# Stages behind a scan start at its second block of channels and load block by block; the last image's stage joins the list

## The chip, the cores and the metric

The kernel runs on one core of one Trainium2 chip. It computes four images in one launch. The metric is the device time in microseconds (us) of that core, as the median over runs; lower is better. TensorE is called PE here, VectorE DVE, ScalarE ACT, GpSimd POOL, and SyncE SP. SP does no arithmetic: it issues the DMAs.

## The reference

Four layers follow each other. Only layers 0 and 3 hold a scan over the 1024 positions of an image; the layers between are a grouped convolution, a masked attention and a mixture of experts. `x` is (4, 32, 32, 256). Cut to what matters for the change:

```python
# layer 0: 512 channels, 64 states, per image
x = layernorm(src) @ w_in; x = gelu(depthwise_conv3x3(x))
dt = softplus(dt_raw @ w_dt + dt_bias)
def step(h, inp):
    xt, dtt, Bt, Ct = inp
    dA = exp(dtt[:, :, None] * A)
    h = dA * h + (dtt * xt)[:, :, None] * Bt[:, None, :]
    return h, einsum('bdn,bn->bd', h, Ct)
_, ys = scan(step, h0, xs)
y = layernorm(ys + x * D_skip)
out = src + (y @ w_out + b_out)

# layer 3: 512 channels, 16 states, per image; its scan has the same form
y = y_seq * silu(x_gate)
t = t + (y @ W_out + b_out)
t = t + moe(layernorm(t))        # 8 experts, the best two of a token kept
```

The change concerns what stands between the scan and its use: the product with `D_skip` and the projection in layer 0, the product with the gate and the projection in layer 3.

## The kernel before

**Units and blocks.** A scan is cut into four blocks `d` of 128 channels, each into two halves `c` of 64 channels. States and channels together fill the 128 partitions: a unit is a tile of 128 rows by 1024 positions, with two channels of 64 states in layer 0 (64 units to a block, 256 to an image) or eight channels of 16 states in layer 3 (16 and 64). The list `SCANS` runs the eight scans one after the other, image 0 and 1 of layer 0, image 0 of layer 3, image 2 of layer 0, image 1 of layer 3, image 3 of layer 0, images 2 and 3 of layer 3: 1280 units, numbered 0 to 1279 here. `scans` (line 345) is a generator that writes them down: for unit k, SP loads the decay `dA` of unit k + 4 (line 410; two DMAs of 256 KB in layer 0, eight of 64 KB in layer 3, into one of five buffers), PE spreads the inputs of unit k + 1 (`ps_rep`), ACT takes the exponential of unit k + 2, DVE multiplies by B and scans, POOL multiplies by C, and PE sums pairs of units over the states (`ps_y`). When a half is summed, ACT copies it out and SP stores it to DRAM in two DMAs (line 464). When the last half of the last block is stored, the scan is put into the set `done` (line 466).

**Stages.** All other work is written as generators that stand in the list `STAGES` (line 33): `front` (layer 0 up to its scan), `middle` (line 1694: `back0`, layers 1 and 2, and layer 3 up to its scan) and `last` (line 1704: `back3` and the last experts). The third entry names the scan that has to be done first. `advance` (line 507) runs the current stage up to its next `yield`; when none is open it takes the first of the list whose scan is in `done`. Only one stage is open at a time.

**How they are interleaved.** The scheduler's own ordering is switched off while the scans run (`manual_schedule`), so each engine gets its instructions in the order in which Python writes them. After each half of a unit `run` (line 521) calls `advance` up to twice, as long as no engine's estimated clock is ahead of DVE's (`LEAD`, `LAG`, `TICKS`, line 45). The value of a `yield` is a note only: `advance` passes it on, but nothing adds it up. If a scan needs inputs that no stage has produced yet, `need` (line 494) advances stages without a scan until they are there.

**What a stage does behind its scan.** `scanned` (line 754) allocates the tile `y_back` and loads it with eight DMAs of 256 KB. `back0` (line 761) loads the residual `tb` (1 MB), `y_back`, four blocks of `u_back` (512 KB each) and `w_out` (512 KB) one behind the other; after two empty yields POOL adds a bias to `tb`, DVE adds `u * D_skip` to each of the four blocks (the skip instructions), PE transposes `y_back` for the layernorm's sums and then projects it. `back3` (line 1641) does the same with `gate_back` for `u_back`; here POOL multiplies y by the gate in eight pieces, then adds the bias.

**The last image.** Its last stage isn't in the list. When all stages are done, `run` opens a new PSUM pool and writes `last(3)` there, outside `manual_schedule`, so that the scheduler orders it.

**Buffers.** The tiles of the stages come from a stack of pools on the right side of SBUF. A new stage takes the memory of the one that has ended, so its first loads wait for the last readers of that memory, a store to DRAM among them. All loads and stores named here go through SP's one queue, in order.

Of the kernel before, what the change touches and what calls it, by code (L numbers as in the profile page):

```python
# [7 lines left out]
F32 = mybir.dt.float32  # L8
# [5 lines left out]
PSUM = bass.MemoryType.PSUM  # L14
DRAM = bass.MemoryType.DRAM

P = 128
NB = 4
L = 1024
TB = L // P  # L20
C = 256
DI = 512
DC = DI // P
# [9 lines left out]
STAGES = (  # L33
    ("front", 0, None), ("front", 1, None), ("front", 2, None), ("front", 3, None), ("middle", 0, (0, 0)),
    ("middle", 1, (0, 1)), ("middle", 2, (0, 2)), ("middle", 3, (0, 3)), ("last", 0, (3, 0)),
    ("last", 1, (3, 1)), ("last", 2, (3, 2)),
)
SAFE = 40.0
SORTS = 2
AHEAD = 12  # L40
# [49 lines left out]
class Metered:  # L90
# [21 lines left out]
    def __getattr__(self, key):  # L112
        got = getattr(self.what, key)
        if self.name is None:
            return Metered(got, self.clock, key) if key in self.COST else got
        cost = self.COST[self.name].get(key)
        if cost is None:
            return got

        def run(*args, **kw):  # L120
            self.clock[self.name] += cost(*args, **kw)
            return got(*args, **kw)  # L122

        return run


class Hybrid:
# [217 lines left out]
    def scans(self, mp, psum):  # L345
# [7 lines left out]
        nc = self.nc  # L353
# [9 lines left out]
        y = None  # L363
# [77 lines left out]
        def pair(k):  # L441

            nonlocal y
            scan, d, c, i, j = units[k]
            n = self.states[scan[0]]
            per = 32 * n // P
            collect = self.tables[scan[0]][2]
            if i == 0:
                y = psum.tile([P, 512], F32, tag="y", name="ps_y", bufs=1)
            h = [state.pop(k - 1), state.pop(k)]  # L450
            for g in range(2):
                for j in range(2):
                    at = 32 * (2 * g + j)
                    nc.tensor.matmul(
                        y[at : at + 32, :], lhsT=collect[:, i, :],
                        rhs=h[j][:, g * 512 : (g + 1) * 512],
                        start=(i == 0), stop=(i == per - 1), tile_position=(0, at),
                    )
            if i == per - 1:
                yo = mp.tile([P, 512], F32, tag="yo", name="yo", bufs=2)  # L460
                nc.scalar.copy(yo, y)
                to = self.keep(("y", *scan, d, c), [64, L])
                for g in range(2):
                    nc.sync.dma_start(to[:, g * 512 : (g + 1) * 512], yo[64 * g : 64 * g + 64, :])
                if d == DC - 1 and c == 1:
                    self.done.add(scan)

        for k in range(AHEAD):
            chunk(k)
# [37 lines left out]
    def advance(self):  # L507

        if self.stage is None:
            can = [x for x in self.todo if x[2] is None or x[2] in self.done]  # L510
            if not can:
                return None
            self.todo.remove(can[0])
            self.stage = getattr(self, can[0][0])(can[0][1])
        cost = next(self.stage, None)
        if cost is None:
            self.stage = None
            return 0.0
        return cost

    def run(self):

        self.done, self.ready = set(), set()
        self.todo, self.stage = list(STAGES), None
        nc, tc = self.nc, self.tc
        with tc.tile_pool(name="scan", bufs=1) as mp, tc.tile_pool(
            name="scps", bufs=1, space=PSUM
        ) as psum, tc.tile_pool(name="sdps", bufs=1, space=PSUM) as side, tc.manual_schedule():
            self.side_psum(side)
            self.mask_work, self.sorted = self.mask_prepare(), False  # L530
            clock = self.clock = dict.fromkeys(Metered.COST, 0.0)
            self.nc = Metered(nc, clock)
            for n, _ in enumerate(self.scans(mp, psum)):
                if n % 2:
                    next(self.mask_work, None)
                now = clock["vector"]
                for e in clock:
                    clock[e] = max(clock[e], now - LAG)
                for _ in range(TICKS):
                    if max(clock.values()) > clock["vector"] + LEAD or self.advance() is None:  # L540
                        break
            while self.advance() is not None:
                pass
            self.nc = nc
        assert not self.todo
        with tc.tile_pool(name="lps", bufs=2, space=PSUM) as pp:
            self.side_psum(pp)
            for _ in self.last(NB - 1):
                pass

# [198 lines left out]
    def image(self, flat, b):  # L751
        return flat[b * L : (b + 1) * L, :].rearrange("(j p) c -> p j c", p=P)

    def scanned(self, pool, key):
        y = pool.tile([P, DC, L], F32, name="y_back")
        for d in range(DC):
            for c in range(2):
                self.nc.sync.dma_start(y[64 * c : 64 * c + 64, d, :], self.mem["y", *key, d, c])
        return y

    def back0(self, b, tb):

# [1 line left out]
        nc, tc, vec = self.nc, self.tc, self.vec  # L764
        with tc.tile_pool(name=f"k{b}", bufs=1, side="right") as sp:
            nc.sync.dma_start(tb, self.image(self.a["x"].rearrange("b h w c -> (b h w) c"), b))
            y = self.scanned(sp, (0, b))
            u = sp.tile([P, DC, L], F32, name="u_back")
            for d in range(DC):
                nc.sync.dma_start(u[:, d, :], self.mem["u", 0, b, d])  # L770
            w_out = sp.tile([P, DC, C], F32, name="w_out0")
            nc.sync.dma_start(w_out, self.mem[("w_out0",)])
            yield 2.0
            yield 2.0
            yield from self.add_rows(tb, self.bout0, TB)
            for d in range(DC):
                nc.vector.scalar_tensor_tensor(
                    y[:, d, :], u[:, d, :], vec["L0_conv_D_skip"][:, d : d + 1], y[:, d, :],
                    ALU.mult, ALU.add,
                )  # L780
                yield 1.3
            mv = sp.tile([P, TB, 2], F32, name="b0mv")
            got = {}

# [856 lines left out]
    def back3(self, b, tb):  # L1641
        nc, tc = self.nc, self.tc
        with tc.tile_pool(name=f"h{b}", bufs=1, side="right") as sp:
            nc.sync.dma_start(tb, self.mem["t", b])
            y = self.scanned(sp, (3, b))
            gate = sp.tile([P, DC, L], F32, name="gate_back")
            for d in range(DC):
                nc.sync.dma_start(gate[:, d, :], self.mem["gate", b, d])
            w_out = self.weight(sp, "L3_attn_W_out", DC)
            yield 2.0  # L1650
            yield 2.0
            for d in range(DC):
                for g in range(2):
                    cols = slice(g * 512, (g + 1) * 512)
                    nc.gpsimd.tensor_tensor(y[:, d, cols], y[:, d, cols], gate[:, d, cols], ALU.mult)
                    yield 0.8
            yield from self.add_rows(tb, self.bout3, TB)
            got = {}

            def project(j):  # L1660
# [95 lines left out]
```

## Time and profile before

| What | Value |
|---|---|
| median of 3 runs | 6912.75 us (6912.15 to 6918.07) |
| the profiled execution's own time | 6914.57 us |
| its span, first to last instruction | 6912.9 us |
| granted TensorE clock, mean | 0.822 |
| DVE busy in 3847 to 3893 us (scan alone) | 43.41 of 46 us |
| DVE busy in 3893 to 3925 us (a middle stage begins) | 18.65 of 32 us, DMA engines 0.91 busy |
| SP's loads of `dA` | 2048 of 256 KB and 2048 of 64 KB |
| last instruction of the scans ends | about 6480 us |

A page of the profile gives busy time and instruction counts by engine over the span of one execution. A timeline line gives start and length in us, the engine, the line of the code, the operation, what it writes and reads, the shapes, how many instructions are merged, and in brackets how long the engine had stood idle before it and what ended that. `SPq` lines are DMAs being issued; when their data lands is not in them. Line 122 stands for everything that goes through the wrapper that keeps the estimated clocks, so most of the work carries it, and the tiles' names tell the instructions apart. In the list of waits at a tile, a line gives the releaser, the idle time in us and how often it occurred.

### The profile page before, as it was taken

Reading aid. Unit: us, or ns where it says so; the run is one execution under the profiler, and the core shown is the slowest. Engines: PE = TensorE matmul, PEld = TensorE weight load, DVE = VectorE, ACT = ScalarE, POOL = GpSimd, SP = SyncE. Lnnn points to the kernel's source line nnn. Section 1 sums busy time; section 2 is a strip of 40 time slices with the busy share of each in tenths; the row PEclk is TensorE's granted clock in tenths of the full one; section 3 lists DMA queues with packets and bytes.
Section 4 is the critical chain, followed back from the end, with each engine's and each line's share of the span. In section 5 each row is a group of like instructions: output and inputs, shape, how many; then the busy total and the mean of one; then the engine's idle time right before and its main releaser. Section 6 shows DMA issues by size and latency. Waiting matters only on the chain. (4 is left out here: it accounts for less than half of the span.)

```text
span 6912.9 us, 66308 instructions
## 1 busy us (share of the span) xinstructions
PE 5388.0 (78%) x20516; PEld 2219.1 (32%) x20516; DVE 5204.9 (75%) x4477; ACT 3440.9 (50%) x4145; POOL 3644.9 (53%) x1801
## 2 busy tenths in 40 slices
PE   6558768678797567879689668798698678867979
PEld 3002212222342032234145322243253322523556
DVE  7778988877898986889889867898899840237411
ACT  2426667345476333457568334477386332244411
POOL 0876776755557654555856545557666530035200
PEclk8568768679898577989789779898698889877989
DMA  1556665654466665446656655456666630145321
GB/s 71 147 147 161 176 173 157 183 134 113 119 173 169 157 164 128 116 126 177 184 142 165 174 135 124 121 150 173 168 165 167 162 95 0 49 123 144 95 61 34
DMA packets 394239, 937.47 MB, mean 136 GB/s; under 512 B 83220, under 2 KB 165729, under 8 KB 392225
## 3 DMA queue, kind: packets, MB, share of 16 engines
q1 hardware_dynamic: 391696, 930.53, 51.1%
q8 instruction: 172, 2.82, 0.2%
q0 software_dynamic: 2128, 2.13, 0.2%
q14 instruction: 243, 1.98, 0.1%
HBM read 842.59 MB, written 93.95 MB: 135 GB/s over the span
## 5 line engine op out<-in xcount | busy, mean ns | idle before, releaser
L122 POOL TENSOR_TENSOR h<-h,rows 128x1024 f32<-128x1024 f32 x1280 | 3028.5, 2369 | 2002.5 <-DVE h L122 1620.7
L122 DVE TENSOR_TENSOR_SCAN h<-dA,ps_rep 128x1024 f32<-128x1024 f32 x1280 | 2924.6, 2285 | 209.8 <-issue 89.5
L122 DVE TENSOR_TENSOR ps_rep<-ps_rep,rows 128x1024 f32<-128x1024 f32 x1280 | 1553.3, 1213 | 336.3 <-PE ps_rep L122 313.8
L122 ACT ACTIVATE dA<-dA,A_L_conv_A_log 128x1024 f32<-128x1024 f32 x1024 | 1152.3, 1145 | 693.0 <-DMA dA<-dt 582.1
L122 PE MATMUL ps_rep<-S,spread_L_conv_A_log 96*128 96x512 bf16 x2048 | 755.7, 459 | 751.9 <-DVE h L122 696.0
L122 PE MATMUL ps_y<-h,collect_L_conv_A_log 128*32 128x512 f32 x4096 | 774.0, 750 | 104.3 <-POOL h L122 104.2
L122 ACT ACT_TABLE_LOAD x486 | 623.5, 1283 | 72.4 <-PE ps_h L122 49.9
L122 PEld LDWEIGHTS <-spread_L_conv_A_log 96*128 96x128 bf16 x2048 | 164.3, 103 | 1502.8 <-DVE h L122 1157.5
L122 PE MATMUL ps_h<-xTm,we 128*128 128x512 f32 x1280 | 605.7, 609 | 5.6 <-ACT h_m L122 4.5
L122 PE MATMUL ps_e<-we,h_m 128*128 128x256 f32 x2560 | 589.1, 382 | 6.8 <-ACT h_m L122 6.8
L122 ACT ACTIVATE p<-ps_sc 128x512 f32<-128x512 f32 x512 | 277.9, 594 | 588.7 <-PE ps_sc L122 558.6
L122 PEld LDWEIGHTS ps_e<-we,h_m 128*128 128x128 f32 x2560 | 483.2, 190 | 137.1 <-issue 46.7
L122 ACT ACTIVATE dA<-dA,A_L_attn_A_log 128x1024 f32<-128x1024 f32 x256 | 293.4, 1148 | 460.6 <-DMA dA<-dt 434.6
L122 PE MATMUL ps_at<-p,v 128*32 128x512 f32 x1024 | 361.6, 624 | 61.4 <-ACT p L122 53.3
L122 PE MATMUL ps_rep<-S,spread_L_attn_A_log 96*128 96x512 bf16 x512 | 188.8, 458 | 266.5 <-DVE h L122 220.9
L122 ACT ACTIVATE h_m<-ps_h,cols 128x512 f32<-128x512 f32 x320 | 217.0, 687 | 313.2 <-PE ps_h L122 310.4
L122 DVE SCALAR_TENSOR_TENSOR tb<-ps_e,cw,tb 128x256 f32<-128x256 f32 x448 | 192.6, 473 | 214.4 <-PE ps_e L122 214.4
L122 PEld LDWEIGHTS ps_h<-xTm,we 128*128 128x128 f32 x1280 | 242.5, 194 | 287.0 <-issue 238.7
L122 PE MATMUL ps_sc<-qT,kT 32*128 32x512 f32 x1024 | 301.8, 665 | 0.0
L122 PE MATMUL ps_at<-p,ones 128*32 128x512 f32 x1024 | 278.7, 624 | 0.0
L122 PE MATMUL ps_cv<-pad,diag 128*128 128x512 f32 x576 | 260.4, 593 | 0.0
L122 PEld LDWEIGHTS ps_y<-h,collect_L_conv_A_log 128*32 128x32 f32 x4096 | 101.3, 119 | 488.5 <-POOL h L122 240.3
(360 smaller groups left out, 5454.3 us busy)
## 6 DMA issues: line engine op xcount, KB each, us to landing
dA<-dt SPq DMA_DIRECT2D x2048, 256.0 KB
dA<-dt SPq DMA_DIRECT2D x2048, 64.0 KB
we<-in_L_ffn_W_dram SPq DMA_DIRECT2D x64, 512.0 KB
parts<-parts SPq DMA_DIRECT2D x64, 384.0 KB
S<-parts SPq DMA_DIRECT2D x96, 256.0 KB
dt<-sp_r SPq DMA_DIRECT2D x64, 256.0 KB
y<-yo SPq DMA_DIRECT2D x128, 128.0 KB
y_back<-y SPq DMA_DIRECT2D x64, 256.0 KB
```

The source lines that it names most:

```text
L122: return got(*args, **kw)
```

## The change

Five things are edited.

1. `done` takes a pair of scan and block when the second half of a block is stored, for every block.
2. `advance` looks for a stage whose scan has its last block done, and failing this for one whose scan has block `EARLY` = 1 done, so two blocks of four.
3. `scanned` no longer allocates; it loads one block (two DMAs), after it has yielded a `Wait` for that block. While a `Wait` isn't fulfilled, `advance` returns None and runs nothing, other stages included.
4. `back0` and `back3` load block by block: the block of u or gate, then the two y loads, then the product of the block before. The bias on `tb` comes right after the first block, `w_out` is loaded there too. Four yields stand between a block's loads and the product of the block before.
5. `last` of image 3 joins `STAGES`, and the separate ending of `run` is gone, with its PSUM pool.

```diff
@@ -33,8 +33,10 @@
 STAGES = (
     ("front", 0, None), ("front", 1, None), ("front", 2, None), ("front", 3, None), ("middle", 0, (0, 0)),
     ("middle", 1, (0, 1)), ("middle", 2, (0, 2)), ("middle", 3, (0, 3)), ("last", 0, (3, 0)),
-    ("last", 1, (3, 1)), ("last", 2, (3, 2)),
+    ("last", 1, (3, 1)), ("last", 2, (3, 2)), ("last", 3, (3, 3)),
 )
+
+EARLY = 1
 SAFE = 40.0
 SORTS = 2
 AHEAD = 12
@@ -122,6 +124,10 @@
             return got(*args, **kw)
 
         return run
+
+
+class Wait(tuple):
+    pass
 
 
 class Hybrid:
@@ -462,8 +468,8 @@
                 to = self.keep(("y", *scan, d, c), [64, L])
                 for g in range(2):
                     nc.sync.dma_start(to[:, g * 512 : (g + 1) * 512], yo[64 * g : 64 * g + 64, :])
-                if d == DC - 1 and c == 1:
-                    self.done.add(scan)
+                if c == 1:
+                    self.done.add((scan, d))
 
         for k in range(AHEAD):
             chunk(k)
@@ -507,21 +513,29 @@
     def advance(self):
 
         if self.stage is None:
-            can = [x for x in self.todo if x[2] is None or x[2] in self.done]
+            can = [
+                x for d in (DC - 1, EARLY) for x in self.todo
+                if x[2] is None or (x[2], d) in self.done
+            ]
             if not can:
                 return None
             self.todo.remove(can[0])
             self.stage = getattr(self, can[0][0])(can[0][1])
+        if self.wait and self.wait not in self.done:
+            return None
+        self.wait = None
         cost = next(self.stage, None)
         if cost is None:
             self.stage = None
             return 0.0
+        if isinstance(cost, Wait):
+            self.wait = tuple(cost)
         return cost
 
     def run(self):
 
         self.done, self.ready = set(), set()
-        self.todo, self.stage = list(STAGES), None
+        self.todo, self.stage, self.wait = list(STAGES), None, None
         nc, tc = self.nc, self.tc
         with tc.tile_pool(name="scan", bufs=1) as mp, tc.tile_pool(
             name="scps", bufs=1, space=PSUM
@@ -543,10 +557,6 @@
                 pass
             self.nc = nc
         assert not self.todo
-        with tc.tile_pool(name="lps", bufs=2, space=PSUM) as pp:
-            self.side_psum(pp)
-            for _ in self.last(NB - 1):
-                pass
 
 
 
@@ -751,12 +761,11 @@
     def image(self, flat, b):
         return flat[b * L : (b + 1) * L, :].rearrange("(j p) c -> p j c", p=P)
 
-    def scanned(self, pool, key):
-        y = pool.tile([P, DC, L], F32, name="y_back")
-        for d in range(DC):
-            for c in range(2):
-                self.nc.sync.dma_start(y[64 * c : 64 * c + 64, d, :], self.mem["y", *key, d, c])
-        return y
+    def scanned(self, key, y, d):
+
+        yield Wait((key, d))
+        for c in range(2):
+            self.nc.sync.dma_start(y[64 * c : 64 * c + 64, d, :], self.mem["y", *key, d, c])
 
     def back0(self, b, tb):
 
@@ -764,21 +773,34 @@
         nc, tc, vec = self.nc, self.tc, self.vec
         with tc.tile_pool(name=f"k{b}", bufs=1, side="right") as sp:
             nc.sync.dma_start(tb, self.image(self.a["x"].rearrange("b h w c -> (b h w) c"), b))
-            y = self.scanned(sp, (0, b))
+            y = sp.tile([P, DC, L], F32, name="y_back")
             u = sp.tile([P, DC, L], F32, name="u_back")
-            for d in range(DC):
+            w_out = sp.tile([P, DC, C], F32, name="w_out0")
+
+            def fetch(d):
                 nc.sync.dma_start(u[:, d, :], self.mem["u", 0, b, d])
-            w_out = sp.tile([P, DC, C], F32, name="w_out0")
-            nc.sync.dma_start(w_out, self.mem[("w_out0",)])
-            yield 2.0
-            yield 2.0
-            yield from self.add_rows(tb, self.bout0, TB)
-            for d in range(DC):
+                yield from self.scanned((0, b), y, d)
+
+            def skip(d):
                 nc.vector.scalar_tensor_tensor(
                     y[:, d, :], u[:, d, :], vec["L0_conv_D_skip"][:, d : d + 1], y[:, d, :],
                     ALU.mult, ALU.add,
                 )
+
+            yield 1.0
+            yield from fetch(0)
+            yield from self.add_rows(tb, self.bout0, TB)
+            nc.sync.dma_start(w_out, self.mem[("w_out0",)])
+            for d in range(1, DC):
+                yield from fetch(d)
+                for _ in range(4):
+                    yield 0.5
+                skip(d - 1)
                 yield 1.3
+            for _ in range(4):
+                yield 0.5
+            skip(DC - 1)
+            yield 1.3
             mv = sp.tile([P, TB, 2], F32, name="b0mv")
             got = {}
 
@@ -1642,19 +1664,31 @@
         nc, tc = self.nc, self.tc
         with tc.tile_pool(name=f"h{b}", bufs=1, side="right") as sp:
             nc.sync.dma_start(tb, self.mem["t", b])
-            y = self.scanned(sp, (3, b))
+            y = sp.tile([P, DC, L], F32, name="y_back")
             gate = sp.tile([P, DC, L], F32, name="gate_back")
-            for d in range(DC):
+
+            def fetch(d):
                 nc.sync.dma_start(gate[:, d, :], self.mem["gate", b, d])
-            w_out = self.weight(sp, "L3_attn_W_out", DC)
-            yield 2.0
-            yield 2.0
-            for d in range(DC):
+                yield from self.scanned((3, b), y, d)
+
+            def gated(d):
                 for g in range(2):
                     cols = slice(g * 512, (g + 1) * 512)
                     nc.gpsimd.tensor_tensor(y[:, d, cols], y[:, d, cols], gate[:, d, cols], ALU.mult)
                     yield 0.8
+
+            yield 1.0
+            yield from fetch(0)
+            w_out = self.weight(sp, "L3_attn_W_out", DC)
             yield from self.add_rows(tb, self.bout3, TB)
+            for d in range(1, DC):
+                yield from fetch(d)
+                for _ in range(4):
+                    yield 0.5
+                yield from gated(d - 1)
+            for _ in range(4):
+                yield 0.5
+            yield from gated(DC - 1)
             got = {}
 
             def project(j):
```

## The prediction

> **What bounds the kernel now.** I read the page first, then the waits at the tile `y_back` (the summed scan output that a stage loads back), then the timelines around each of its loads, and last the order in which the two built programs put instructions on each engine.
>
> ```profile
> PE 5388.0 (78%) x20516; PEld 2219.1 (32%) x20516; DVE 5204.9 (75%) x4477; ACT 3440.9 (50%) x4145; POOL 3644.9 (53%) x1801
> ```
>
> No engine is full over the span. The shape is a serial scan of 1280 units on DVE, each a multiply (1.21 us) and a scan (2.29 us), start to start 3.60 us where nothing else is on DVE (3887.08 to 3890.68). A unit that comes late is never caught up there, so idle DVE inside the scan is end-to-end time, up to unit 1210 (5663 us), where image 3's middle stage runs without a scan (488 us between units 1210 and 1211), and again from 6151 us to the scan's end.
>
> The list of waits at `y_back` names the idle time that the change aims at:
>
> ```profile
>   DMA u_back<-u: 54.7, 4
>   DMA gate_back<-gate: 51.6, 4
> ```
>
> Middle stage of image 2, DVE and then SP's own queue:
>
> ```profile
> 3894.28 2.29 DVE L122 TENSOR_TENSOR_SCAN h<-dA,ps_rep 128x1024 f32<-128x1024 f32 x1 [0.19 <-ACT dA L122]
> 3896.48 1.21 DVE L122 TENSOR_TENSOR ps_rep<-ps_rep,rows 128x1024 f32<-128x1024 f32 x1
> 3910.78 2.51 DVE L122 SCALAR_TENSOR_TENSOR y_back<-u_back,cols,y_back 128x1024 f32<-128x1024 f32 x2 [13.09 <-DMA u_back<-u]
> ```
> ```profile
> 3893.80 1.11 SPq L464 DMA_DIRECT2D y<-yo  x2
> 3895.00 0.53 SPq L766 DMA_DIRECT2D tb<-in_x_dram  x1
> 3895.63 6.10 SPq L758 DMA_DIRECT2D y_back<-y  x8
> 3902.30 3.42 SPq L770 DMA_DIRECT2D u_back<-u  x4
> 3906.44 0.32 SPq L772 DMA_DIRECT2D w_out<-w_out  x1
> 3907.52 4.78 SPq L410 DMA_DIRECT2D dA<-dt  x5
> ```
>
> The reader is to see one block of 14 loads (5.5 MB), and DVE standing on it 13.09 us in the middle of the scan. The other three middle stages stand 13.89, 13.14 and 14.55 us; the four make the 54.7. A last stage does the same through POOL: it waits for its gates with the scan's own products queued behind, PE then waits for these, and DVE for PE:
>
> ```profile
> 3421.37 2.48 POOL L122 TENSOR_TENSOR y_back<-y_back,gate_back 128x512 f32<-128x512 f32 x2 [14.79 <-DMA gate_back<-gate]
> 3429.14 1.23 DVE L122 TENSOR_TENSOR ps_rep<-ps_rep,rows 128x1024 f32<-128x1024 f32 x1 [10.76 <-PE ps_rep L122]
> 6229.36 2.29 DVE L122 TENSOR_TENSOR_SCAN h<-dA,ps_rep 128x1024 f32<-128x1024 f32 x1 [17.07 <-DMA dA<-dt]
> ```
>
> Image 0 costs DVE 10.76 us, image 1 9.45, image 2 17.07. The seven stalls sum to 54.67 + 37.28 = 92 us, 1.3% of the span: the most that smoother loading can bring.
>
> [...] the `dA` loads issued at 3850.12 move only after the 1 KB packets of the output store issued before them (3854 to 3858.2 in the packet records). [...] So SP stands still, with all loads behind it; below, `tb` is issued 5.4 us after the output store. [...] After each middle start SP issues 344 DMAs from 3907 to 4093 us, one per 0.54 us.
>
> **The change part by part.** Profiled span 6912.9 us; that execution took 6914.57, the median is 6912.75.
>
> *Where stages start.* By the two instruction orders, middle stages 0 to 3 begin at units 254, 465, 822 and 1142 instead of 257, 513, 833 and 1153. After block 2 they block, with nothing run in their place (nothing else was ready then before either). In images 1 to 3 transposes, projection and all that follows stand behind the same units as before; image 0's stage runs 4 to 5 units later, into a stretch (460 to 513) where the scan was alone: no cost. Last stages 0 to 2 start where they did. The last one starts after the scan in both orders, since stage 2 holds the place until then: the edit of the stage list changes no overlap.
>
> *Removed at a middle start.* Only two y loads remain behind the last store, and two of the four skip instructions (1.28 us each) have already run in the old scan; they cost there what they save here. The last y load must wait for its store. Store issued 3893.80, its packets gone by 3898, load landed near 3901; DVE is there at 3901.2 (scan, skip, multiply, scan after 3894.28). So about 1 us of the 13 to 14 remains.
>
> *Added at the early start.* 5 MB now lie beside the scan. Units take 0.5 MB each (two `dA` of 256 KB per 3.6 us, 145 GB/s), the packet records show 240 to 260 GB/s for such rows and near 400 for whole 128-row tiles, and five `dA` buffers give some 10 us of cover. For images 0 and 1 I followed SP and DVE unit by unit: each skip comes one to four units after its load, and no wait over 1 us appears. Image 0: 13.89 - 1 = 13. Image 1: 13.14 - 2 = 11.
>
> Images 2 and 3 are worse. Their start comes directly behind a last stage, whose output store reads the same `tb`:
>
> ```profile
> 3849.49 0.53 SPq L1709 DMA_DIRECT2D out_dram<-tb  x1
> 3850.12 11.23 SPq L410 DMA_DIRECT2D dA<-dt  x8
> ```
>
> In the new order `tb`, u0 and y0 stand behind one more `dA` pair, so SP waits from 3851 until the store has landed, about 3858.2; the next `dA` pair goes out near 3861 instead of 3853 (its scan is due at 3868, so it is just in time), y0 lands near 3868, and DVE wants it at 3861.4: 6.6 us, and about 2.5 more at the second skip. I take 9. Image 2: 13.09 - 9 = 4; image 3: 14.55 - 9 - 1 = 5 (bounds -3 and 12 each: the first if SP, which then issues eight DMAs per unit, does not catch up; the second if the store lands as fast as in the empty tail).
>
> *Last stages 0 to 2.* Same loads in four portions with `dA` pairs between; POOL adds the bias first, which needs only `tb`. At image 0 `tb` lands near 3410 instead of the gate at 3421, and each product follows its load by two units. 10.76 - 1 = 10, 9.45 - 0.5 = 9. At image 2 a unit takes eight DMA issues of 0.46 us, so the 13 loads still cost SP some 6.5 us: 17.07 - 9 = 8 (bounds 3 and 14).
>
> *The tail.* PE's order is the same from end to end.
>
> ```profile
> 6610.84 0.38 SPq L1709 DMA_DIRECT2D out_dram<-tb  x1
> 6616.26 0.34 SPq L1644 DMA_DIRECT2D tb<-t  x1
> ```
> ```profile
> 6638.43 13.26 PE L1665 MATMUL ps_o<-w_L_attn_W_out,y_back 128*128 128x256 f32 x58 [0.48 <-POOL y_back L1655]
> ```
>
> Two y loads used to slip in during the 5.4 us wait and now stand behind it; gates and y's land last near 6637 and the first projection stays where it is (+0.5). Statistics no longer alternate with the additions: six of eight pairs at 0.52 us move behind the last addition, +3.2. One activation table load of 1.28 us leaves the path. Sum +2 (bounds -2, +6).
>
> Sum: 13 + 11 + 4 + 5 + 10 + 9 + 8 - 2 = 58 us. 6912.75 - 58 = **6855 us**.
>
> **The rivals.**
> - *More comes out.* The store wait is covered by prefetched units, and SP keeps up: images 2 and 3 give 12 each, last stage 2 gives 14: 58 + 15 + 6 = 79, 6834 us. For it: two units of slack at each skip. Against: POOL's bias additions also wait for that `tb`.
> - *SP keeps half.* Behind middle starts 1 to 3 and last stage 2 the scan runs on units of eight DMAs, and SP issues without a pause for 186 us. Then what counts is not DVE's idle time but the 12 issues fewer: image 1 gives 5, images 2 and 3 -2 each, last stage 2 gives 3: 13 + 5 - 4 + 10 + 9 + 3 - 2 = 34, 6879 us.
> - *No change.* Later waits take the time back, as PE is up to 97% busy in some slices (5011 to 5184 us): within 10 us of before. Against: the stalls stand in scan-only or loading stretches where PE is idle too.
> - *Slower.* The block is moved, not hidden. 5 MB queue ahead of `dA` behind the same five buffers, so DVE stands 13.7 us at each early start as it did at the late one, plus 8 at images 2 and 3 for the store and 3 at each late y load: 4 x 16.7 + 16 = 83 against 54.7 removed, last stages gain nothing as their bytes are the same, tail +2: +30, 6943 us. It decides from about 19 us of new stall per image, since the last stages' 27 us must be eaten too.
>
> **How the numbers follow.** Forecast 0.48, more 0.15, SP keeps half 0.22, no change 0.08, slower 0.07. The likeliest gives 6855; its own range is 6842 to 6868. The range of 6832 to 6888 takes in the first rival and most of the second and leaves out about 0.2. About 0.2%, 14 us, is what this measurement can tell from no change: faster 0.86, same 0.07, slower 0.07.
>
> **What would show it.** In the changed profile: no wait of DVE over 3 us for `u_back` at the late starts; DVE waits for `y_back` or `u_back` of 5 to 9 us beginning some 10 units earlier in images 2 and 3 alone, with SP standing about 7 us before `tb`; POOL's wait for `gate_back` under 5 us outside the tail; a tail from the end of PE's last `ps_e` of image 2 to the end that is 2 us longer. Early waits above 15 us in images 0 and 1, or `dA` waits that grow by what the skips lose, would make the prediction wrong.

## The result, and the profile after

| What | Before | After |
|---|---|---|
| median of the runs (8 each) | 6915.41 us | 6898.60 us (6883.87 to 6911.96) |
| ratio, with 95% interval | | 0.9974 (0.9962 to 0.9985) |
| span of the profiled execution | 6912.9 us | 6902.1 us |

The change saves about 17 us (0.26%, between 0.15 and 0.38%); 58 were forecast. The two profiled executions, of which views are shown below, lie 10.8 us apart.

The first part of the page of after: busy time, share of the span, instructions. The work is the same. Line 124 is here what line 122 was in the kernel before, and `...` stands for lines left out.

```profile
PE 5422.5 (79%) x20516; PEld 2221.7 (32%) x20516; DVE 5209.3 (75%) x4477; ACT 3437.1 (50%) x4143; POOL 3649.9 (53%) x1801
```

What POOL's gate product waits for, from the view of the tile `gate_back`: us in total, then times.

```profile
  DMA y_back<-y: 22.3, 10
```

The 51.6 us for the gate that stood there are gone; what is left is ten waits for y, the longest, 5.91 and 4.35 us, at image 2. At the first last stage the products now follow their loads (POOL's timeline of after):

```profile
3425.55 1.28 POOL L124 TENSOR_TENSOR y_back<-y_back,gate_back 128x512 f32<-128x512 f32 x1
...
3434.11 1.27 POOL L124 TENSOR_TENSOR y_back<-y_back,gate_back 128x512 f32<-128x512 f32 x1 [1.44 <-DMA y_back<-y]
```

Middle stage of image 2, DVE's timeline of after, its four skip instructions:

```profile
3859.03 3.46 DVE L124 SCALAR_TENSOR_TENSOR y_back<-u_back,cols,y_back 128x1024 f32<-128x1024 f32 x1 [7.37 <-DMA y_back<-y]
...
3869.18 2.69 DVE L124 SCALAR_TENSOR_TENSOR y_back<-u_back,cols,y_back 128x1024 f32<-128x1024 f32 x1 [0.88 <-DMA y_back<-y]
...
3900.59 1.26 DVE L124 SCALAR_TENSOR_TENSOR y_back<-u_back,cols,y_back 128x1024 f32<-128x1024 f32 x1
...
3908.54 1.28 DVE L124 SCALAR_TENSOR_TENSOR y_back<-u_back,cols,y_back 128x1024 f32<-128x1024 f32 x1 [3.08 <-DMA y_back<-y]
```

The late stall of 13.09 us has shrunk to 3.08, and a new one of 7.37 stands 11 units earlier. At image 3 it is 4.26 late and 6.25 early, at image 0 a wait of 1.06, and at image 1 none above 0.8. DVE's waits in front of the skips sum to 22.9 us, worked out from the trace, against 54.7 in before. SP's timeline of after shows the wait in front of `tb` (3841.65 to 3849.73), behind the output store:

```profile
3839.82 0.53 SPq L1743 DMA_DIRECT2D out_dram<-tb  x1
3840.45 1.20 SPq L416 DMA_DIRECT2D dA<-dt  x2
3849.73 0.40 SPq L775 DMA_DIRECT2D tb<-in_x_dram  x1
3850.22 0.53 SPq L781 DMA_DIRECT2D u_back<-u  x1
3850.80 1.17 SPq L768 DMA_DIRECT2D y_back<-y  x2
```

Since both traces hold the same 1280 scans, the time from unit to unit can be set side by side. Worked out from the starts of the scans in both traces (us); each column is one execution:

| Units | What lies there | Before | After | Difference | Forecast |
|---|---|---|---|---|---|
| 254 to 465 | middle stage, image 0 | 979.2 | 993.7 | +14.5 | -13 |
| 465 to 544 | start of the middle stage, image 1 | 329.4 | 318.1 | -11.3 | -11 |
| 716 to 822 | last stage, image 0 | 449.0 | 439.9 | -9.1 | -10 |
| 822 to 870 | start of the middle stage, image 2 | 219.5 | 219.4 | -0.1 | -4 |
| 1036 to 1142 | last stage, image 1 | 446.8 | 437.6 | -9.2 | -9 |
| 1142 to 1210 | middle stage, image 3 | 350.1 | 346.2 | -3.9 | -5 |
| 1211 to 1279 | last stage, image 2 | 326.8 | 328.8 | +2.0 | -8 |
| after 1279 | last stage, image 3 | 434.8 | 439.7 | +4.9 | +2 |
| the rest | | 3377.3 | 3378.7 | +1.4 | 0 |

One row carries most of the miss: image 0 was to gain 13 us and lost 14.5. Small rows say little: units 0 to 254, the same in every kernel here, take 1061 to 1066 us in the seventeen traces. "The rest" also holds such differences, +4.4, -6.3 and +5.1 us among them.

### The profile page after: what moved, and what is told of

The parts are those of the page before. It is cut to its first block, busy times and chain, and to the rows that moved or that the text cites. A ratio compares the mean times of both kernels' runs of the same rounds, so it can differ in the third digit from the quotient of the medians.

```text
span 6902.1 us, 66302 instructions
## 1 busy us (share of the span) xinstructions
PE 5422.5 (79%) x20516; PEld 2221.7 (32%) x20516; DVE 5209.3 (75%) x4477; ACT 3437.1 (50%) x4143; POOL 3649.9 (53%) x1801
## 5 line engine op out<-in xcount | busy, mean ns | idle before, releaser
L124 PE MATMUL ps_h<-xTm,we 128*128 128x512 f32 x1536 | 718.1, 607 | 4.3 <-ACT h_m L124 3.2
L124 PE MATMUL ps_e<-we,h_m 128*128 128x256 f32 x3072 | 702.1, 381 | 8.7 <-ACT h_m L124 8.7
L124 PEld LDWEIGHTS ps_e<-we,h_m 128*128 128x128 f32 x3072 | 580.5, 190 | 158.9 <-issue 54.0
L124 DVE SCALAR_TENSOR_TENSOR tb<-ps_e,cw,tb 128x256 f32<-128x256 f32 x512 | 220.6, 474 | 407.4 <-PE ps_e L124 407.4
L124 ACT ACTIVATE h_m<-ps_h,cols 128x512 f32<-128x512 f32 x384 | 260.7, 687 | 487.5 <-PE ps_h L124 484.6
L124 PEld LDWEIGHTS ps_h<-xTm,we 128*128 128x128 f32 x1536 | 291.8, 193 | 339.7 <-issue 289.7
```

## The experiments

All ratios are against runs of the kernel before on the same chip, beside it in time; 0.1% is 7 us. "The separate ending" is that of the kernel before, with `last(3)` outside the list.

**1 and 2. The ending alone, and everything but the ending.** The kernel before with this edit:

```diff
-    ("last", 1, (3, 1)), ("last", 2, (3, 2)),
+    ("last", 1, (3, 1)), ("last", 2, (3, 2)), ("last", 3, (3, 3)),
...
-        with tc.tile_pool(name="lps", bufs=2, space=PSUM) as pp:
-            self.side_psum(pp)
-            for _ in self.last(NB - 1):
-                pass
```

> The kernel before with last(3) in the list and no separate ending; nothing else changed, so up to the scan's end the order is that of the kernel before. Theory A (the new ending costs what the changed kernel's trace shows after the last scan, 5 us): +3 to +7 us. Rival (the ending is neutral, the 5 us were noise): -2 to +2 us. Its trace is also a second look at the old order: theory S (image 0's stage is longer in the new order because of the order) wants image 0's attention at 298 +- 3 us, as in the kernel before, and 978 +- 5 us from unit 254 to unit 465; theory N (the attention's length varies from one execution to the next) allows 298 to 314 us.

and the changed kernel with the same edit reversed:

> The changed kernel with the separate ending of the kernel before. Theory A: 5 us faster than the changed kernel, about 22 us faster than before (ratio 0.9968). Rival (ending neutral): 17 us faster than before (0.9975). Second look at the new order: theory S wants image 0's attention at 309 +- 3 us and 994 +- 5 us from unit 254 to unit 465; theory N allows 298 to 314 us.

Measured: 1.0005 (0.9995 to 1.0015), so +3 us with an interval that holds zero; and 0.9963 (0.9950 to 0.9975). By these ratios alone theory A and its rival can't be told apart. The traces speak for A: behind unit 1279 the five with the new ending (after and experiments 1, 3, 7 and 8) take 438.3 to 439.9 us, the twelve with the separate one 426.8 to 435.9.

The traces also speak for theory S: image 0's attention took 299.2 us in the old order (298.1 in before) and 315.1 in the new one (309.2 in after), units 254 to 465 took 977.8 and 1000.5 us. The last two figures of the new order lie above the ranges that S had named, so its size varies, but image 0's loss is no accident of one execution.

**3. No early start.** The changed kernel with

```diff
-EARLY = 1
+EARLY = DC - 1
```

> The changed kernel with EARLY = DC - 1: stages load block by block, but start only when the whole scan is summed. Theory B (loading block by block removes the stalls by itself, the early start only moves loads behind the output store's wait and shifts image 0's work): the late stalls fall below 5 us in each image, no early stall of 10 to 14 us at images 2 and 3, so 20 to 45 us faster than the changed kernel (ratio to before 0.990 to 0.995). Rival (the early start is what removes the stall, since two blocks less must be loaded late): late stalls of 8 us or more at each image, the same time as the changed kernel or slower (0.997 to 1.000).

Measured: 1.0097 (1.0083 to 1.0112), 67 us slower than before; neither side had that. Theory B fell: the first skip of each image still waits 5.43, 7.23, 8.27 and 8.88 us, later ones wait again, and the waits above 0.8 us sum to 60 us, worked out from the trace, against 54.7 in before. The rival was right on these waits, but 5 us more of them don't make 67. In this kernel all four middle stages stand 5 units behind their old places (by the traces image 1's experts start in unit 637 instead of 632), where the changed kernel has only image 0 so. Experiment 8 returns to this.

**4. The last stages alone.** The kernel before with `back3` of the changed kernel:

> The kernel before with only back3 loading block by block (an empty yield stands where the changed kernel waits for a block); middle stages and the ending are those of before. Forecast: 10 + 9 + 8 = 27 us faster (ratio 0.9961). Theory P (behind image 2 the scan is bound by SP's issues and gives the gain back): 10 + 10 + 2 = 22 us or less (0.9968 or above). Rival C (the gain of the last stages is given back in the mixture of experts that follows): within 8 us of before.

Measured: 0.9955 (0.9943 to 0.9967), 31 us faster, against 27 forecast. By the two ratios that is 13 us more than the whole change brings (the intervals just overlap), so the middle stages together with the ending bring no gain. Yet image 2's last stage gives nothing here either (332 us from unit 1211 to 1279, 327 in before). DVE's timeline of after shows it:

```profile
6221.33 2.29 DVE L124 TENSOR_TENSOR_SCAN h<-dA,ps_rep 128x1024 f32<-128x1024 f32 x1 [4.20 <-DMA dA<-dt]
...
6236.50 2.29 DVE L124 TENSOR_TENSOR_SCAN h<-dA,ps_rep 128x1024 f32<-128x1024 f32 x1 [4.22 <-DMA dA<-dt]
...
6247.26 0.69 DVE L124 TENSOR_TENSOR tb<-ps_o,tb 128x512 f32<-128x512 f32 x1 [7.35 <-PE ps_o L124]
```

One stall of 17.07 us has become several, and the wait for the projection, 4.87 us in before, is now 7.35. SP's timeline of after points to the reason:

```profile
6227.26 8.78 SPq L416 DMA_DIRECT2D dA<-dt  x16
...
6237.73 13.51 SPq L416 DMA_DIRECT2D dA<-dt  x24
```

With a gate and two y loads in between, SP issues one DMA behind the other here, without a gap, while the DMA engines are busy for 0.64 to 0.79 of the time (by tens of us, 6220 to 6250). So it looks as if the number of issues holds this stage and not the bytes; no run separates them.

**5. The delay alone.** The kernel before, loads and skips untouched, with empty yields in `middle`, first 20 and then 18:

```diff
             yield from self.back0(b, tb)
+            for _ in range(20 if b == 0 else 0):
+                yield 0.5
             yield from self.layer1(b, tb)
```

> The kernel before, with 20 empty yields between back0 and layer1 of image 0 and no other edit: from layer 1 of image 0 to the end of its middle stage the work stands behind the same units as in the changed kernel, and loads, skips and all other images are those of before. Theory S (the place of image 0's stage relative to the scan's units decides[...]): attention of image 0 at 309 to 316 us instead of 298, unit 473 later than in the kernel before by 15 to 25 us, total +10 to +25 us (ratio 1.0015 to 1.0036). The forecast's step (4 to 5 units later into a stretch where the scan was alone: no cost): attention 298 us, total within 5 us of before.

> The kernel before with 18 empty yields between back0 and layer1 of image 0 instead of the 20 of the run before: layer 1 and all that follows in image 0 stand 4 units behind their old place instead of 5, so that each step of the attention again begins at an odd unit (305 to 367, old 301 to 363; with 20 yields 306 to 368). Theory O (odd or even decides: the scan's sums on TensorE come every second unit, and only in the old parity does the stage's work fit between them): attention of image 0 at 297 to 301 us, total within 6 us of before (ratio 0.9991 to 1.0009). Theory D (any later place costs): attention 305 to 316 us, +15 to +26 us (1.002 to 1.004).

| Empty yields | Image 0's attention stands at units | It takes | Ratio |
|---|---|---|---|
| 0 (before) | 301 to 363 | 298.1 us | 1 |
| 18 | 305 to 367 | 299.3 us | 1.0000 (0.9991 to 1.0009) |
| 20 | 306 to 368 | 305.5 us | 1.0038 (1.0025 to 1.0052) |

The units are those of the scan beside which the attention is written in program order; a place is called odd when its first unit is odd. Four units later costs nothing, five units later costs 26 us. Theory O holds, D falls. Of theory S the place is right. The clock isn't the cause: with 20 yields PE pauses 1.62 and 1.50 us at two places in the attention, but no drop of the clock follows either, and the granted clock is the same with 18 and with 20 yields (0.94 in the attention, 0.85 and 0.84 in units 368 to 465). So the 26 us are not the clock's; its drops come on top (experiment 7).

What the parity (odd or even) does is seen where the attention meets the scan. With 18 yields, PE and DVE:

```profile
1542.69 1.13 PE L122 MATMUL ps_sc<-qT,kT 32*128 32x512 f32 x4
...
1544.41 0.60 PE L122 MATMUL ps_rep<-S,spread_L_conv_A_log 96*128 96x512 bf16 x2
...
1544.93 1.07 PE L122 MATMUL ps_y<-h,collect_L_conv_A_log 128*32 128x512 f32 x8
...
1545.04 1.23 DVE L122 TENSOR_TENSOR ps_rep<-ps_rep,rows 128x1024 f32<-128x1024 f32 x1 [0.18 <-PE ps_rep L122]
```

With 20 yields:

```profile
1544.52 1.09 PE L122 MATMUL ps_y<-h,collect_L_conv_A_log 128*32 128x512 f32 x7
...
1545.55 1.13 PE L122 MATMUL ps_sc<-qT,kT 32*128 32x512 f32 x4
...
1547.26 0.60 PE L122 MATMUL ps_rep<-S,spread_L_conv_A_log 96*128 96x512 bf16 x2
...
1547.90 1.23 DVE L122 TENSOR_TENSOR ps_rep<-ps_rep,rows 128x1024 f32<-128x1024 f32 x1 [1.04 <-PE ps_rep L122]
```

The scan's sums `ps_y` come once in two units. In the odd places they stand behind the `ps_rep` that DVE needs next; in the even places `ps_y` and the scores `ps_sc` both stand in front of it, and DVE waits 1.04 us instead of 0.18. Two units take 4.10 + 3.89 us in the one and 4.75 + 3.89 in the other. This goes on for some ten units and returns in another form later; in between the pairs take as long in both. The experts and layer 3 behind it pay too: units 368 to 465 take 426.7 us in before, 429.2 with 18 yields, 446.6 with 20 and 446.7 in after. How the order brings this about there wasn't followed instruction by instruction. Over units 254 to 465 the traces differ by 14 us (981.1 with 18 yields, 995.3 with 20), so some 12 of the 26 us aren't placed.

Of the odd-numbered shifts only 5 was run. That every second unit is bad is argued from this view; a shift of 3 or 6 would test it.

**6. The same cure in the changed kernel.** Both kernels have the separate ending. The first has image 0's stage in its old place, with the loads of the old `back0` for it:

```diff
-                if x[2] is None or (x[2], d) in self.done
+                if x[2] is None or (x[2], d) in self.done and (d == DC - 1 or x[1] in (1, 2, 3))
```

The second keeps image 0 as changed, with two yields fewer:

```diff
-            for _ in range(4):
+            for _ in range(2 if b == 0 else 4):
                 yield 0.5
             skip(DC - 1)
```

> The changed kernel with the old separate ending, and with image 0's middle stage starting and loading as before (one block of loads after its whole scan); images 1 to 3 and the last stages as changed. Theory S: attention of image 0 back at 298 us, image 0's late stall of 14 us back, and 10 to 18 us faster than the changed kernel with the old ending (ratio to before 0.994 to 0.995). The forecast's step (13 us are gained at image 0): 13 us slower than that kernel (0.998).

> The changed kernel with the old separate ending, and at image 0 two empty yields instead of four in front of the last skip, so that from layer 1 on image 0's work stands one unit earlier and at odd units again; loads and skips as changed. Theory O: attention of image 0 at 297 to 301 us, unit 473 at 2278 to 2284 us instead of 2297 to 2303, 15 to 24 us faster than the same kernel with four yields, ratio to before 0.993 to 0.994, so at least as fast as with image 0 in its old form. Theory D: within 5 us of the kernel with four yields (0.9955 to 0.997).

Measured: 0.9939 (0.9926 to 0.9953) and 0.9930 (0.9917 to 0.9943), against 0.9963 with the four yields. Two empty yields are worth about 23 us. In the second, image 0's attention takes 297.1 us again. From unit 254 to 465 it takes 967.5 us, 11.7 fewer than before: the stall's end was worth about what was forecast, once the stage stands in an odd place.

**7. Keeping TensorE's clock up.** A second loss in image 0's attention is the clock that PE is granted. Three stretches of 10 us in image 0's attention of after (columns: window, length, busy time of PE, PE's weight loads, DVE, ACT and POOL, then the granted clock, DMA share and GB/s), and PE's instruction at 1751.26:

```profile
1742.00:1752.00 10.00, 8.50 (x47) 2.14 (x44) 8.51 (x5) 7.11 (x10) 4.27 (x3) 0.95 0.33 80
1752.00:1762.00 10.00, 9.68 (x32) 2.00 (x31) 6.02 (x4) 1.09 (x2) 6.39 (x3) 0.54 0.60 157
1762.00:1772.00 10.00, 9.90 (x62) 3.05 (x64) 7.98 (x5) 5.77 (x9) 3.35 (x2) 1.00 0.21 52
```
```profile
1751.26 1.04 PE L124 MATMUL ps_rep<-S,spread_L_conv_A_log 96*128 96x512 bf16 x2 [1.50 <-DVE h L124]
```

A pause of 1.50 us is followed by 10.24 us at half the clock; in these 10 us 32 matmuls run, 47 and 62 in those beside them. In the odd places the pause at the same step is 1.07 us, and no drop follows it in the traces of before and of five experiments. In the even places the attention took 305.5 us where no drop followed the two pauses (20 yields), 309.2 with one of 10.24 us (after) and 315.1 with one of 13.65 and one of 10.24 (experiment 2).

If the pauses bring the drops (theory G), filling them has to keep the clock up. The two scores in front of them were computed twice in the changed kernel (the second result replaces the first):

```diff
+            if self.image_now == 0 and hp == 2 and kb == 1:
+                for i in range(2):
+                    nc.tensor.matmul(
+                        two[i], lhsT=kT[rows[i], c, kb * P : (kb + 1) * P], rhs=qT[rows[i], c, qs],
+                        start=True, stop=True,
+                    )
```

> The changed kernel with two useless matmul pairs (a score product written twice, the second time by the real one) in front of the scores of the two places in image 0's attention where PE paused 1.73 and 1.50 us; the result is the same. Theory G [...]: pauses there of 1.1 us or less, no drop of the granted clock at these two places, the four steps behind the second one in 17 us instead of 21, attention some 3 us shorter than 309 although PE has more to do. Rival (the drop has another cause[...]): the drop stays, attention 1 to 2 us longer.

It settled nothing: PE's pause in front of that `ps_rep` grew to 2.30 us, worked out from the ends and starts of PE's instructions; the clock dropped all the same, and the attention took 323 us. The pause of 1.73 us near its first third was gone, but another had grown from 4.18 to 9.54. So pauses were moved and not filled. Its one time was 6902.77 us.

**8. The late start with the parity mended.** Experiment 3, with two yields instead of four in front of the last skip of every image:

> The changed kernel with EARLY = DC - 1, as in the first such run (+67 us against before), and with two empty yields instead of four in front of the last skip of each image: the middle stages of all four images then stand 4 units behind their old places instead of 5, at odd units again. Theory O (odd or even decides, in every image): 60 to 95 us faster than that run, ratio to before 0.996 to 1.001. Theory D (the late start itself costs, some 6 us for each unit of delay): 8 to 25 us faster than that run, ratio 1.006 to 1.009.

Measured: 0.9972 (0.9961 to 0.9984), 86 us faster than with four. Four units against five decides in the other images too: by the traces the four middle stages (units 254 to 465, 544 to 716, 870 to 1036, 1142 to 1211) give 25, 22, 18 and 10 us. So the 67 us of experiment 3 were not the cost of starting late. The stalls are still there (65 us of waits above 0.8 us in front of the skips): to take them away the early start is needed.

**9. The early stalls of images 2 and 3.** In three steps. First, the changed kernel with the separate ending and `tb` loaded later:

```diff
+                if d == 2 and b >= 2:
+                    load_tb()
                 yield from fetch(d)
```

with its bias additions behind the second skip at images 2 and 3.

> The changed kernel with the old separate ending; in middle stages 2 and 3 the load of tb and its bias addition stand before and after the third block instead of in front of the first, so that the first loads do not stand behind the wait for the output store. Theory T (the early stalls of 14 and 11 us at images 2 and 3 come from SP's wait for that store): these stalls fall below 5 us, 15 to 20 us faster than with tb in front (ratio to before 0.9935 to 0.9945). Rival (the early stalls come from the bytes of the loads themselves, as at image 1, or from another wait on the same memory): stalls stay at 8 us or more, within 6 us of that kernel (0.9955 to 0.997).

Measured: 0.9967 (0.9959 to 0.9975), no gain over 0.9963; theory T fell. SP no longer waits in front of the first loads, DVE does all the same:

```profile
3862.51 0.80 SPq L788 DMA_DIRECT2D u_back<-u  x1
3863.45 1.55 SPq L772 DMA_DIRECT2D y_back<-y  x2
```
```profile
3877.51 1.28 DVE L124 SCALAR_TENSOR_TENSOR y_back<-u_back,cols,y_back 128x1024 f32<-128x1024 f32 x1 [8.71 <-DMA y_back<-y]
```

DVE goes on 13 us after the second of the two y loads was issued at 3864.56, and the stall is 8.71 us instead of 7.37. The same edit together with image 0 in its old form:

> Both edits together: image 0 as before, tb late at images 2 and 3, the old ending. Theories S and T: 25 to 38 us faster than the changed kernel with the old ending, ratio to before 0.991 to 0.993. Only S: 0.994 to 0.995; only T: 0.9935 to 0.9945; neither: 0.9963.

Measured: 0.9957 (0.9943 to 0.9971), no faster than image 0's old form alone (0.9939, 0.9926 to 0.9953).

Second, the skips moved behind their loads by empty yields, with image 0 in its old form:

```diff
-                    for _ in range(4):
+                    for _ in range((0, 16, 8, 4)[d]):
```

> Image 0 as before, the old ending, and at images 1 to 3 sixteen and eight empty yields instead of four and four in front of the first two skips, which then stand some 3 units behind their loads and still in front of the wait for the last block; the rest of the order is that of the kernel with image 0 in its old form. Theory Y (the early stalls of 14 and 11 us are skips that wait for bytes which land 10 to 12 us after their issue; later skips do not wait): units 822 to 833 in 42 to 46 us instead of 53.6, units 1142 to 1153 in 42 to 46 instead of 51, and 12 to 22 us faster than that kernel (ratio 0.991 to 0.992). Rival (the bytes also hold up dA, so the scan stalls instead of the skip): the two stretches stay above 49 us, no gain.

Measured: 0.9942 (0.9927 to 0.9956), no gain over 0.9939. Units 822 to 833 and 1142 to 1153 take 48.7 and 47.4 us, between the two forecasts, but the late skips then wait 6.62 and 6.39 us instead of 3.28 and 4.03. At image 2 DVE no longer waits at the early skip but for PE, PE for POOL, and POOL for `tb`, in that kernel's POOL timeline:

```profile
3839.28 3.70 POOL L124 TENSOR_TENSOR tb<-tb,row_L_conv_b_out 128x512 f32<-128x512 f32 x3 [9.60 <-DMA tb<-in_x_dram]
```

Third, both. The base is a new version: the changed kernel with the separate ending, image 0 mended, and at images 1 to 3 three blocks loaded and skipped in front of the wait for the last one, so that the stage also stands 2 units earlier.

```diff
+                if b == 0 or d < DC - 1:
                     yield from fetch(d)
-                for _ in range(4):
+                for _ in range(12 if b and d == 1 else 4):
                     yield 0.5
                 skip(d - 1)
                 yield 1.3
-            for _ in range(4):
+            if b:
+                yield from fetch(DC - 1)
+            for _ in range(2):
                 yield 0.5
             skip(DC - 1)
```

> The changed kernel with the old ending and two empty yields fewer in image 0, and at images 1 to 3 the loads and skips of three blocks in front of the wait for the last block, so that only one block's loads and its skip stand behind the scan and the stage runs 2 units earlier, at odd units. If the late block is what is left of the late stalls: 5 to 20 us faster than the kernel with image 0 alone mended, ratio 0.990 to 0.9925. If the early bytes cost what the late ones save: 0.9925 to 0.9945.

Measured: 0.9912 (0.9896 to 0.9927), median 6855.81 us, the lowest ratio of all, though its interval overlaps that of 0.9930. The number lies where the late block was to be what is left, but the waits don't agree: the late skips of images 1 to 3 still wait 6.36, 6.84 and 8.80 us. Image 2's start is no shorter in it either (61.2 us from unit 822 to 833, 53.7 in after). It gains behind that, as from unit 1162 to 1211, where image 3's stage ends, 715.7 us instead of 732.1 in after; why wasn't found. With `tb` late at images 2 and 3, and four more yields in front of the first skip there:

> The kernel of the run before (three blocks early, image 0 mended, old ending), and at images 2 and 3 the load of tb behind the second block with its bias additions on POOL behind the second skip, and four more empty yields in front of the first skip. Theory W (two waits lie over each other at these early starts: the skip that waits for y, and POOL's bias that waits for tb behind the output store, with the scan's products queued behind it; each hid the other when one alone was moved): with both moved, units 822 to 833 fall from 61 us to 44 to 50 and units 1142 to 1153 from 59 to 44 to 50, ratio to before 0.9865 to 0.989. Rival (the bytes of three blocks hold up dA whatever the order): the stretches stay at 55 us or more, ratio 0.9905 to 0.993.

Measured: 0.9925 (0.9907 to 0.9942), no faster; units 822 to 833 and 1142 to 1153 take 59.8 and 55.3 us. Theory W fell, the rival holds. With the wait at the first skip and POOL's wait for `tb` gone, DVE stands on the decay itself, and further on still on the last y load:

```profile
3821.59 2.29 DVE L124 TENSOR_TENSOR_SCAN h<-dA,ps_rep 128x1024 f32<-128x1024 f32 x1 [4.74 <-ACT dA L124]
...
3832.96 2.29 DVE L124 TENSOR_TENSOR_SCAN h<-dA,ps_rep 128x1024 f32<-128x1024 f32 x1 [5.50 <-ACT dA L124]
...
3881.74 1.28 DVE L124 SCALAR_TENSOR_TENSOR y_back<-u_back,cols,y_back 128x1024 f32<-128x1024 f32 x1 [8.73 <-DMA y_back<-y]
```
```profile
3820.36 1.15 ACT L124 ACTIVATE dA<-dA,A_L_conv_A_log 128x1024 f32<-128x1024 f32 x1 [18.27 <-DMA dA<-dt]
3831.72 1.15 ACT L124 ACTIVATE dA<-dA,A_L_conv_A_log 128x1024 f32<-128x1024 f32 x1 [10.22 <-DMA dA<-dt]
```

The DMA engines have no gap there: their busy share is 1.04 from 3812 to 3844 us, at 263 GB/s, and 1.04 at image 2's early start in after (3852 to 3880). So the bytes that the early start puts beside the scan's own, behind an output store, delay `dA` or y in each of the orders tried.

## Why the prediction was wrong

- **The step that failed** is in "Where stages start": "image 0's stage runs 4 to 5 units later, into a stretch (460 to 513) where the scan was alone: no cost". The stretch was there, but it was the wrong question. Side work and scan share PE in a pattern of two units, and whether it is 4 units or 5 decides. With four (18 yields) the sentence is true, with five (20 yields) it costs 26 us; the changed kernel has five, and two yields taken out of it give 23 back. On top come drops of the clock, 4 to 10 us of the attention in the traces (309.2 and 315.1 us against 305.5 without one), which the prediction didn't have.
- **The stalls at images 0 and 1** were sized rightly: -11.7 (with the parity mended) and -11.3 us, against 13 and 11.
- **Images 2 and 3**: an early stall of 9 us was foreseen, out of SP's wait for the store, and SP does wait 8 us. But that wait isn't its cause: with it gone the stall is as long, with the DMA engines busy throughout. The stretches 822 to 833 and 1142 to 1153 grew by 13.8 and 10.7 us, 2.6 of each being skips moved there, and the late waits are 3.08 and 4.26 us instead of about 1. So they gain 0.1 and 3.9 us, not 4 and 5. The rival "slower" had the mechanism right here, that the block is moved and not hidden, but at two images and not at four.
- **Last stages**: images 0 and 1 as forecast (-9.1, -9.2). The third gave nothing instead of 8: the term "17.07 - 9" was mis-sized, and the stall came back as several shorter waits for `dA` and `ps_o`. For this one stage the rival "SP keeps half" was closer, and SP's timeline agrees with its reason. Its working is too wide in one place: SP issues 344 DMAs in 186 us behind middle starts 1 and 2 and 341 behind 3, but 91 behind the first.
- **The ending** costs 4.9 us between the traces of before and after and 3 by experiment 1, with an interval that holds zero; 2 were forecast.
- **The forecast sum** of 58 us assumed that nothing but the waits counts. With the parity mended and the old ending, 0.9930 is 48 us; the forecast for that would have been 60.

"No change" was given 0.08, within 10 us of before, for another reason, later waits that take the time back as PE is full. Much of the time was taken back, but in the same stage's own work and not at a later limit.

## What to carry to other kernels

Where two streams of work are written into one static order, moving one of them by a unit can cost more than the stall that the move removes: compare the new offset with the period of the other stream, and try a unit more and a unit fewer before judging the change. An edit that looks bad as a whole may be a good edit in a bad phase, as 67 us slower became 19 us faster by two empty yields per image. A stall seen at a load may have a second wait of about the same length behind it, and behind both the bytes; take away each wait in turn, and both together, before calling one of them the cause.

## What the runs showed of the hardware

In the traces of before and after, the clock that PE is granted is 1.0 or 0.5 and nothing else. Before has 104 stretches at 0.5, together 2460 of its 6913 us; after has 100, together 2501 of its 6902 us. They last from 3.41 to 239 us in before and from 3.41 to 167 us in after.

In image 0's attention a drop follows some of PE's pauses and not others:

| Trace | PE's pause | Clock behind it |
|---|---|---|
| before, in front of the `ps_rep` at 1731.58 | 1.07 us | stays at 1.0 |
| after, in front of the `ps_rep` at 1588.56 | 1.73 us | stays at 1.0 |
| after, in front of the `ps_rep` at 1751.26 | 1.50 us | 0.5 for 10.24 us |
| 20 yields (experiment 5) | 1.62 and 1.50 us | no drop |

The pause of 1.73 us in after, near the attention's first third, stands at the same instruction as one in experiment 2; there the clock fell to 0.5 for 13.65 us behind it. So between 1.50 and 1.73 us the length of a pause alone doesn't tell whether a drop follows. What decides it was not shown by these runs.
